# Two square feed-forward layers as seven half-size products instead of eight, in float32 on one Trainium2 core

## The chip, the core and the metric

The kernel runs on one NeuronCore of a Trainium2 chip. The core has five engines with a queue each: TensorE (PE, matrix products into PSUM), VectorE (DVE), ScalarE (ACT), GpSimd (POOL) and SyncE (SP, here only an issuer of DMAs). PE's weight loads have a row of their own in the profile (PEld). The metric is the device time of one execution in microseconds, median over runs.

## What is computed

One transformer block on x of 4 batches x 1024 tokens x 256 features, everything in float32. First attention with 16 heads of 16, its output normalised and added to x. Then the feed-forward part, which the change is about:

```python
def _tlin(x, w, s):
    return jnp.einsum('bsi,oi->bso', x, w) * s
h = jax.nn.silu(_tlin(x, w1_w, w1_s)) * _tlin(x, w2_w, w2_s)      # 256 -> 1024
h = jax.nn.gelu(_tlin(h, h1_w, h1_s), approximate=False)          # 1024 -> 1024
h = jax.nn.gelu(_tlin(h, h2_w, h2_s), approximate=False)          # 1024 -> 1024
return _tlin(h, w3_w, w3_s)                                       # 1024 -> 256
...
x = x + _layernorm(_L0_ffn_ref(_layernorm(x, axis=-1), ...), axis=-1)
```

The weights of these layers are drawn from -1, 0 and 1; the scales `*_s` are real, one per output feature. h1 and h2 are the two square layers.

## The kernel before

**Two programs.** `tile_fast` computes everything on two assumptions, that the attention scores are bounded and that the weights survive a rounding; it counts violations in `misses`, and if there is one, `tile_general` computes all again. With the inputs here the flag stays zero.

**Numbers in two halves.** [...] So an activation is split into a high part (the rounded value) and a low part (what is left), and each product is made twice, with the high and the low part, into the same PSUM accumulator. The weights are rounded once: `round_weights` (L241) loads a block of a weight matrix on POOL's DMA queue, casts it on POOL and stores it to a DRAM copy `rounded`, during attention. Later `check_weights` and `count` (L905, L916) load the original weights again, compare them on DVE with the rounded ones in SBUF and count differences; `judge` (L930) adds the counts up with a 1-column matmul on PE.

**Order.** The schedule is manual: every engine runs its instructions in the order in which the program writes them. Attention is a loop over score tiles (`exponentials`, L464, and `weigh`, L474). Work beside it is cut into `Step`s, kept in chains of the object `side`; each call of `side.take()` (L638) lets each chain run the steps that are due, where `gap` is the number of calls since the chain's last step.

**Feed-forward.** `feed_forward` (L945) goes over the eight half batches of 512 tokens, features on the partitions:
- `gated` (L816): for each of 8 blocks of 128 features, 8 matmuls for w1 and w2, then silu on ACT (L828), the product on DVE (L830), the split on ACT and DVE (L818, L819).
- `gelu_layer` (L838), once for h1 and once for h2: for each pair of output blocks, 8 input blocks x 2 x (high, low) = 32 matmuls through `product` (L812 to L814), then per block of 128 x 512 one gelu on ACT from PSUM (L850), a cast and a difference on DVE (L851, L852). Results go from one pair of buffers (`ha`) to the other (`hb`) and back.
- `finish` (L854): 64 matmuls of 256 columns with w3 (L867), scaled on DVE (L869). Its normalisation and the store to DRAM are a chain of steps taken during the next half batch.
- `prepare` (L782): the norm of the next half batch and its transposes on PE, in steps during h1 and h2.

All of h1, h2, w1, w2 and w3 stay in SBUF for the whole feed-forward part: h1 in the tiles that held attention's stacks, h2 and w3 where attention's other buffers were (`load_weights`, L755; `open_ffn`, L759). PSUM has three buffers of 128 x 1024 for the products, one for attention's accumulator, one for small things.

Of the kernel before, what the change touches and what calls it, by code (L numbers as in the profile page):

```python
# [39 lines left out]
TPQ = NQ // P  # L40

# [76 lines left out]
def tile_fast(ctx: ExitStack, tc: tile.TileContext, x, wqk, wv, wo, w1, w1s, w2, w2s, h1, h1s, h2, h2s, w3, w3s, out, bad):  # L118
# [46 lines left out]
    blocks = [(n, c) for n, w in weights.items() for c in range(0, w.shape[0] // P, rows_at_once[n])]  # L165
    counts = sum(w.shape[0] * w.shape[1] for w in weights.values()) // (P * NQ)
    misses = const.tile([P, counts + B * 2], F32, name="misses")
    nc.vector.memset(misses, 0.0)
    rounded = {n: dram.tile(list(w.shape), F32R, name=f"{n}_r") for n, w in weights.items()}
# [11 lines left out]
    with ExitStack() as actx, ExitStack() as rctx:  # L181
# [62 lines left out]
        def round_weights(n, c):  # L244
# [15 lines left out]
            return [Step(load, 2, False), Step(cast, 4, False)]  # L260

# [439 lines left out]
        def unit_end(b, g, h):  # L701
# [19 lines left out]
            if b == B - 1 and g == NG - 2:  # L721
                side.add([Step(lambda c=c: load_weights("h1", [c]), 2 if c else 0, False) for c in range(HC // 2)])
# [8 lines left out]
            if g == NG - 3 and b + 1 < B:  # L731
                later["chain"][0].extend(later["rest"])
            elif g == NG - 3:
                chunks = [(n, [c]) for n in ("w1", "w2") for c in range(DC)]
                loads = [Step(lambda n=n, c=c: load_weights(n, c), 2 if n == "w1" else 1, False) for n, c in chunks]

                loads[0].ready = lambda: not later["flags"][0]
                loads[DC].ready = lambda: not outstanding
                side.add(loads)
                side.add([Step(lambda: None, 7, False)] + prepare(0, to_vector))  # L740
# [5 lines left out]
        x_in = [t.rearrange("p (c n) -> p c n", c=DC) for t in spare[0:2]]  # L746
        homes = {"w1": spare[2:4], "w2": spare[4:6], "h1": [stacks[w, i, u] for i in range(2) for u in range(2) for w in range(2)]}
        homes["w3"] = [t[:, D * j : D * (j + 1)] for t in spare[6:8] for j in range(HC // 2)]
        halves_of = [(b, h) for b in range(B) for h in range(NH)]
        ffn = {}  # L750

        def halves(pool, name):
            return [pool.tile([P, HC, NQ], F32R, name=f"{name}_{k}") for k in ("hi", "lo")]
# [4 lines left out]

        def open_ffn():  # L759
# [3 lines left out]
            ffn["b"] = halves(fb, "hb")  # L763
            homes["h2"] = [fb.tile([P, HID], F32R, name=f"h2_{c}") for c in range(HC)]
            load_weights("h2")
            load_weights("w3")

# [14 lines left out]
        def prepare(n, copy):  # L782
# [16 lines left out]
            def transposes(c):  # L799
                def run():  # L800
# [3 lines left out]
                    hi, lo = (t[:, c, :] for t in x_in)  # L804
# [7 lines left out]
        def product(p, n, m, i, c):  # L812
            for k, half in enumerate(i):
                nc.tensor.matmul(p, homes[n][c][:, m * P : (m + 1) * P], half[:, c, :], start=c == 0 and k == 0, stop=c == len(homes[n]) - 1 and k == 1)  # L814

        def gated(o, every):  # L816
            def split(m, sg):
                nc.scalar.copy(o[0][:, m, :], sg)  # L818
                return lambda: nc.vector.tensor_sub(o[1][:, m, :], sg, o[0][:, m, :].bitcast(F32))  # L819

            before = None
            for m in range(HC):
                p = ps.tile([P, 2, NQ], F32, tag="big", name="pg")
                for k, n in enumerate(("w1", "w2")):
                    for c in range(DC):
                        product(p[:, k, :], n, m, x_in, c)
                sg = both.tile([P, NQ], F32, tag="o", name="sg", bufs=2)
                nc.scalar.activation(sg, p[:, 0, :], AF.Silu, scale=scales["w1"][:, m : m + 1])  # L828
                low = split(*before) if before else None
                nc.vector.scalar_tensor_tensor(sg, p[:, 1, :], scales["w2"][:, m : m + 1], sg, ALU.mult, ALU.mult)  # L830
                if low:
                    low()
                before = m, sg
                if m % every == every - 1:
                    side.take()
            split(*before)()

        def gelu_layer(o, i, n):  # L838

            for m0 in range(0, HC, 2):  # L840
                p = ps.tile([P, 2, NQ], F32, tag="big", name="ph")
                for c in range(HC):
                    for j in range(2):
                        product(p[:, j, :], n, m0 + j, i, c)
                    if c % 2:
                        side.take()
                for j in range(2):
                    m = m0 + j
                    a = both.tile([P, NQ], F32, tag="o", name="a", bufs=2)
                    nc.scalar.activation(a, p[:, j, :], AF.Gelu, scale=scales[n][:, m : m + 1])  # L850
                    nc.vector.tensor_copy(o[0][:, m, :], a)  # L851
                    nc.vector.tensor_sub(o[1][:, m, :], a, o[0][:, m, :].bitcast(F32))  # L852

        def finish(n, i):  # L854

            b, h = halves_of[n]
            st = {}
            z = both.tile([P, TPQ, D], F32, tag="y", name=f"z_{n}", bufs=1)

            pairs = [ps.tile([P, 2, NQ], F32, tag="big", name="pz") for _ in range(TPQ // 2)]  # L860
            p = [pairs[t // 2][:, t % 2, :D] for t in range(TPQ)]
            for t0 in range(0, TPQ, 2):
                ts = range(t0, t0 + 2)
                for c in range(HC):
                    for t in ts:
                        for k, half in enumerate(i):
                            nc.tensor.matmul(p[t], half[:, c, t * P : (t + 1) * P], homes["w3"][c], start=c == 0 and k == 0, stop=c == HC - 1 and k == 1)  # L867
                for t in ts:
                    nc.vector.tensor_mul(z[:, t, :], p[t], w3s_sb)  # L869
                if n == len(halves_of) - 1:  # L870

                    ln = norms.stats([z[:, t, :] for t in ts])
                    for j, t in enumerate(ts):
                        norms.apply(z[:, t, :], z[:, t, :], ln, j)
                        nc.vector.tensor_add(z[:, t, :], z[:, t, :], xs[b][:, h * TPQ + t, :])
                        for at, tokens in pieces(h, out[b].rearrange("(t p) d -> p t d", p=P)):
                            k = h * TPQ + t - at.start
                            if 0 <= k < at.stop - at.start:
                                nc.sync.dma_start(out=tokens[:, k, :], in_=z[:, t, :])
            if n == len(halves_of) - 1:  # L880
                return []

            def apply(i0):
                def run():
                    for t in range(i0, i0 + 2):
                        norms.apply(z[:, t, :], z[:, t, :], st["ln"], t)
# [3 lines left out]
            def add(t):  # L890
                def run():
                    nc.vector.tensor_add(z[:, t : t + 2, :], z[:, t : t + 2, :], xs[b][:, h * TPQ + t : h * TPQ + t + 2, :])
# [391 lines left out]
```

## Time and profile before

| | us |
|---|---|
| median of 3 runs (1292.04 to 1293.14) | 1292.86 |
| span of the profiled execution | 1291.6 |
| attention, up to the first `pg` matmul | 617 |
| one half batch of the feed-forward part, 780.7 to 862.4 | 81.7 |
| from the last half batch's first matmul (1197.4) to the end | 94.2 |

How to read it: the span is from the first to the last instruction of one profiled execution. Busy time on PE overlaps between neighbouring matmuls, since they are pipelined, so stage lengths are taken from starts, not from busy times. The counts matter too: 2048 matmuls with the square weights (names `ph`), 512 with w1 and w2 (`pg`), 512 of half width with w3 (`pz`), and in the feed-forward part 128 gelus of 128 x 512 on ACT. The DMA rows: 16 loads and 16 stores of 512 KB on POOL's queue for h1 and h2, and 16 loads of 512 KB from the rounded copies on SP's queue.

### The profile page before, as it was taken

Reading aid. Unit: us, or ns where it says so; the run is one execution under the profiler, and the core shown is the slowest. Engines: PE = TensorE matmul, PEld = TensorE weight load, DVE = VectorE, ACT = ScalarE, POOL = GpSimd, SP = SyncE. Lnnn points to the kernel's source line nnn. Section 1 sums busy time; section 2 is a strip of 40 time slices with the busy share of each in tenths; the row PEclk is TensorE's granted clock in tenths of the full one; section 3 lists DMA queues with packets and bytes.
Section 4 is the critical chain, followed back from the end, with each engine's and each line's share of the span. In section 5 each row is a group of like instructions: output and inputs, shape, how many; then the busy total and the mean of one; then the engine's idle time right before and its main releaser. Section 6 shows DMA issues by size and latency. Waiting matters only on the chain.

```text
span 1291.6 us, 21098 instructions
## 1 busy us (share of the span) xinstructions
PE 1244.4 (96%) x8104; PEld 770.0 (60%) x8104; DVE 729.1 (56%) x1625; ACT 699.2 (54%) x855; POOL 120.2 (9%) x166
## 2 busy tenths in 40 slices
PE   7999999999999999998999999999999999999995
PEld 3333334333333334333788888888888888888885
DVE  3466557765677556755643725637456374463533
ACT  3788788888889888998421413214132141331410
POOL 6211012111121110000000000000000000000000
PEclk8999899999999999999999999999999999999998
DMA  4676644665574654462320000201102011020000
GB/s 130 159 188 161 146 121 119 145 162 122 117 178 117 154 117 100 99 163 85 134 92 1 25 1 1 74 17 41 49 1 66 25 42 49 1 66 9 17 1 20
DMA packets 65679, 107.03 MB, mean 83 GB/s; under 512 B 12960, under 2 KB 39200, under 8 KB 65568
## 3 DMA queue, kind: packets, MB, share of 16 engines
q1 hardware_dynamic: 57680, 80.93, 25.4%
q0 software_dynamic: 7360, 24.12, 6.0%
q8 instruction: 66, 1.08, 0.4%
q10 hardware_dynamic: 528, 0.52, 0.2%
q14 instruction: 45, 0.37, 0.1%
HBM read 48.38 MB, written 23.59 MB: 56 GB/s over the span
## 4 chain that ended last, share of the span: by engine, by line
PE 76%; DVE 10%; ACT 8%; issue 2%; DMA 2%; SPq 1%; ACTq 0%; POOL 0%; POOLq 0%; DVEq 0%
PE ph L814 36%; PE acc L479 13%; PE s L471 8%; ACT e L472 6%; PE pz L867 4%; PE p L265 4%; PE pg L814 3%; PE py L265 2%; PE pv L265 2%; DVE sg L830 2%; DVE top L488 2%; DVE ha_lo L819 1%; DVE st L96 1%; PE po L518 1%; ACT sg L828 1%
## 5 line engine op out<-in xcount | busy, mean ns | idle before, releaser
L472 ACT ACTIVATE e<-s 128x1024 f32<-128x1024 f32 x512 | 482.6, 1035 | 59.4 <-PE s L471 49.7
L479 PE MATMUL acc<-e,vaug 128*32 128x512 f32 x2048 | 256.8, 604 | 1.4 <-POOL vaug L449 1.3
L850 ACT ACTIVATE a<-ph,h_scale 128x512 f32<-128x512 f32 x128 | 81.0, 685 | 301.4 <-PE ph L814 301.4
L471 PE MATMUL s<-sq,sk 64*128 64x512 f32 x1024 | 186.0, 443 | 18.2 <-ACT e L472 13.4
L814 PE MATMUL ph<-hb_hi,h 128*128 128x512 f32 x512 | 199.5, 390 | 0.0
L814 PE MATMUL ph<-hb_lo,h 128*128 128x512 f32 x512 | 199.4, 389 | 0.0
L471 PEld LDWEIGHTS s<-sq,sk 64*128 64x128 f32 x1024 | 86.1, 185 | 139.0 <-ACT e L472 114.6
L488 DVE TENSOR_TENSOR top<-top,e 128x512 f32<-128x512 f32 x192 | 134.8, 702 | 16.0 <-ACT e L472 10.8
L106 POOL TENSOR_TENSOR rstd<-ve,minus_half 128x4 f32<-128x4 f32 (+1 forms) x33 | 38.3, 1162 | 834.9 <-DVE ve L104 834.9
L479 PEld LDWEIGHTS acc<-e,vaug 128*32 128x32 f32 x2048 | 49.3, 109 | 107.1 <-issue 102.8
L814 PEld LDWEIGHTS ph<-hb_lo,h 128*128 128x128 f32 x512 | 96.1, 188 | 20.1
L814 PEld LDWEIGHTS ph<-hb_hi,h 128*128 128x128 f32 x512 | 96.1, 188 | 20.2
L851 DVE CAST ha_hi<-a 128x512 fp32r<-128x512 f32 x64 | 27.1, 423 | 142.7 <-ACT a L850 142.7
L814 PE MATMUL ph<-ha_hi,sq 128*128 128x512 f32 x256 | 101.8, 398 | 0.4
L814 PE MATMUL ph<-ha_lo,sq 128*128 128x512 f32 x256 | 99.8, 390 | 0.0
L814 PE MATMUL ph<-ha_lo,sk 128*128 128x512 f32 x256 | 99.7, 390 | 0.0
L814 PE MATMUL ph<-ha_hi,sk 128*128 128x512 f32 x256 | 99.7, 389 | 0.0
L828 ACT ACTIVATE sg<-pg,w_scale 128x512 f32<-128x512 f32 x64 | 43.3, 688 | 56.0 <-DVE ha_lo L819 45.6
L830 DVE SCALAR_TENSOR_TENSOR sg<-pg,w_scale,sg 128x512 f32<-128x512 f32 x64 | 47.1, 745 | 46.3 <-ACT sg L828 46.1
L851 DVE CAST hb_hi<-a 128x512 fp32r<-128x512 f32 x64 | 27.0, 422 | 71.5 <-ACT a L850 71.5
L265 PE MATMUL p<-xT,wqk_sb 128*32 128x512 f32 x512 | 62.3, 608 | 2.9 <-DVE on L496 1.7
L814 PEld LDWEIGHTS ph<-ha_hi,sq 128*128 128x128 f32 x256 | 48.1, 188 | 13.1 <-DVE sg L830 3.4
(165 smaller groups left out, 1640.7 us busy)
## 6 DMA issues: line engine op xcount, KB each, us to landing
w<-in_h_dram POOLq DMA_DIRECT2D x16, 512.0 KB, 5.6
h_r<-wr POOLq DMA_DIRECT2D x16, 512.0 KB, 3.8
x<-in_h_dram SPq DMA_DIRECT2D x32, 256.0 KB, 2.7
top_d<-top SPq DMA_DIRECT2D x30, 256.0 KB, 2.3
folded<-top_d SPq DMA_DIRECT2D x30, 256.0 KB, 3.3
sk<-ck1hi SPq DMA_DIRECT2D x64, 64.0 KB, 2.7
sk<-ck1lo SPq DMA_DIRECT2D x64, 64.0 KB, 2.9
sq<-cq1hi SPq DMA_DIRECT2D x64, 64.0 KB, 2.6
```

The costliest lines, as they stand in the source:

```text
L106: nc.gpsimd.tensor_tensor(rstd[:, :n], ve[:, :n], self.minus_half[:, :n], ALU.pow)
L265: nc.tensor.matmul(o[j : j + SLOT, :], w[:, j : j + SLOT], i, **flags)
L471: nc.tensor.matmul(s[:, a, :], stacks[1, g % 2, u][r, c * P : (c + 1) * P], stacks[0, g % 2, u][r, h * NQ : (h + 1) * NQ], start=True, sto ...
L472: nc.scalar.activation(pair(k)[:, u], s, AF.Exp)
L479: nc.tensor.matmul(acc[SLOT * i : SLOT * (i + 1), :], vaug[g % 2][:, c, i, :], pair(k)[:, i // 2, i % 2, :], start=c == 0, stop=c == NT - 1)
L488: nc.vector.tensor_max(top, top if c > 1 else pair(k - 2)[:, :, :, 0:P], pair(k)[:, :, :, 0:P])
L814: nc.tensor.matmul(p, homes[n][c][:, m * P : (m + 1) * P], half[:, c, :], start=c == 0 and k == 0, stop=c == len(homes[n]) - 1 and k == 1)
L828: nc.scalar.activation(sg, p[:, 0, :], AF.Silu, scale=scales["w1"][:, m : m + 1])
L830: nc.vector.scalar_tensor_tensor(sg, p[:, 1, :], scales["w2"][:, m : m + 1], sg, ALU.mult, ALU.mult)
L850: nc.scalar.activation(a, p[:, j, :], AF.Gelu, scale=scales[n][:, m : m + 1])
L851: nc.vector.tensor_copy(o[0][:, m, :], a)
L867: nc.tensor.matmul(p[t], half[:, c, t * P : (t + 1) * P], homes["w3"][c], start=c == 0 and k == 0, stop=c == HC - 1 and k == 1)
```

## The change

A square layer is seen as a 2 x 2 matrix of blocks, weights A (512 x 512 each) and activations B (512 features x 512 tokens each), over tiles of 1024 tokens, a whole batch. Seven products of sums of blocks replace the eight products of blocks. With s1 = A21 + A22, s2 = s1 - A11, s3 = A11 - A21, s4 = A12 - s2 there are seven weight factors.

- **Weight factors.** `round_corners` replaces `round_weights` for h1 and h2: 16 blocks, each loaded in two DMAs, three quarters copied and four sums made on POOL, stored as seven factors of 1 MB per layer in DRAM (`factors`). They don't stay in SBUF: `load_factor` brings one factor (two loads of 512 KB on SP's queue) into a ring of `SLOTS` = 4 in the tiles that held h1. It is called after each product for the product four later, 56 times in all.
- **Activations.** Eleven blocks of 128 x 4 x 512 are handed out and returned by a list (`Block`, `free`). `Operand.split(i)` makes high and low parts of half a block, 1024 wide: a copy on ACT and a difference on DVE.
- **A layer** (`layer`): seven products k, each in two groups r of 16 matmuls. Two input sums are made on DVE and two on POOL. Products 0 and 1, products 2, 3 and 4, and products 5 and 6 add up in the same PSUM tile, which is read after each. What follows a group, in this order: `evacuate`, the `steps` (input sums, splits of the later operands), the `after` list (splits of this layer's results for the next), one `side.take()`.
- **Around it.** `gated` and `finish` work on 1024 tokens; the gate's result is kept unsplit and split later. The norms of both halves of the next batch are prepared during the layers of this one. The weights are checked against an int8 copy made on POOL, in blocks of 1024 in two chains after the second batch; `judge` is called before the last batch's `finish`.

```diff
-    blocks = [(n, c) for n, w in weights.items() for c in range(0, w.shape[0] // P, rows_at_once[n])]
+    square = ("h1", "h2")
+    blocks = [(n, c) for n, w in weights.items() if n not in square for c in range(0, w.shape[0] // P, rows_at_once[n])]
+    corners = [(n, c, x) for n in square for c in range(HC // 2) for x in range(2)]
...
+            def plain():
+                r = work.tile([P, WIDE], F32R, tag="wr", name="wr", bufs=1)
+                nc.gpsimd.tensor_copy(r[:, 0:half], st["w"][:, 0:half])
+                nc.gpsimd.tensor_copy(r[:, half : 3 * half], st["w"][:, 2 * half : 4 * half])
+                store(r, 0, 3)
+
+            def sums():
...
+                nc.gpsimd.tensor_tensor(s1, a21, a22, ALU.add)
+                nc.gpsimd.tensor_tensor(s2, s1.bitcast(F32), a11, ALU.subtract)
+                nc.gpsimd.tensor_tensor(s3, a11, a21, ALU.subtract)
+                nc.gpsimd.tensor_tensor(s4, a12, s2.bitcast(F32), ALU.subtract)
+                store(r, 3, 7)
...
+            return [Step(load, 2, False), Step(plain, 3, False), Step(sums, 1, False)]
...
+        order = (0, 1, 4, 5, 2, 3, 6)
+        def load_factor(q):
+            if q >= B * 2 * len(order):
+                return
+            n, k = square[q // len(order) % 2], order[q % len(order)]
+            for i, t in enumerate(ring_of[q % SLOTS]):
+                nc.sync.dma_start(out=t.bitcast(F32), in_=factors[n][k, :, 2 * i : 2 * i + 2, :].bitcast(F32))
...
+            def split(self, i):
+                if i == 0:
+                    self.hi, self.lo = Block("hi", F32R), Block("lo", F32R)
+                hi, lo, raw = (t.part(i) for t in (self.hi, self.lo, self.raw))
+                nc.scalar.copy(hi, raw)
+                nc.vector.tensor_sub(lo, raw, hi.bitcast(F32))
...
+        def layer(q, x, pairs, scale, after, late):
+            b11, b21, b22, b12 = (x[i, j] for i, j in ((0, 0), (1, 0), (1, 1), (0, 1)))
+            t2 = Block("t2")
+            moving = [pairs[0, 0], pairs[1, 0], Operand(t2), Operand(b12), Operand(b21), Operand(b11), Operand(b22)]
...
+            def gelu(o, i, m0, src=None):
+                for j in range(2):
+                    m = HC // 2 * i + m0 + j
+                    nc.scalar.activation(o.t[:, m0 + j, :], (o.t[:, m0 + j, :] if src is None else src[:, j, :]), AF.Gelu, scale=scale[:, m : m + 1])
...
+            def evacuate(k, r, p):
+                m0 = 2 * r
+                if k == 0:
...
+                    nc.scalar.copy(out["s"].part(r), p)
+                elif k == 1:
...
+                    gelu(out[0, 0], 0, m0, p)
+                elif k in (2, 3):
...
+                    nc.vector.tensor_add(out[n].part(r), p, out["s"].part(r))
+                else:
+                    n, i, j = (("s", 1, 0), ("v", 1, 1), ("u", 0, 1))[k - 4]
+                    out[i, j] = out[n]
+                    nc.vector.tensor_add(out[n].part(r), p, out[n].part(r))
+                    gelu(out[n], i, m0)
...
+            make1, make2 = sums(nc.vector, b11, b12, b11), sums(nc.vector, t2, b22, b11)
+            make3, make4 = sums(nc.gpsimd, b12, b22, b12), sums(nc.gpsimd, b21, b21, t2)
+            steps = {-1: [lambda: make1(0), lambda: make2(0)], 0: [lambda: make1(1), lambda: make2(1)]}
+            for g in range(4):
+                steps.setdefault(g, []).append(lambda g=g: (make3, make4)[g // 2](g % 2))
+            for k in range(2, 7):
+                for i in range(2):
+                    steps.setdefault(2 * k - 3 + i, []).append(lambda k=k, i=i: moving[k].split(i))
...
+            for k in range(7):
+                start = k in (0, 2, 5)
+                for r in range(2):
+                    if start:
+                        last[r] = ps.tile([P, 2, NQ], F32, tag="big", name="ph")
+                    p = last[r]
+                    for c in range(HC // 2):
+                        for j in range(2):
+                            w = ring_of[q % SLOTS][c // 2][:, c % 2, (2 * r + j) * P : (2 * r + j + 1) * P]
+                            for n, half in enumerate((moving[k].hi, moving[k].lo)):
+                                nc.tensor.matmul(
+                                    p[:, j, :], w, half.t[:, c, :],
+                                    start=start and c == n == 0, stop=c == HC // 2 - 1 and n == 1, skip_group_check=True,
+                                )
+                    if r:
+                        moving[k].release()
+                        load_factor(q + SLOTS)
+                        q += 1
+                    evacuate(k, r, p)
+                    for run in steps.get(2 * k + r, ()):
+                        run()
+                    for run in after.get(2 * k + r, ()):
+                        run(out)
                     side.take()
...
+                after = splits([(9, 0, 0, 0), (11, 0, 0, 1), (12, 1, 0, 0), (14, 1, 0, 1)])
...
+                x = gated(after)
...
+                if b + 1 < B:
+                    chain[0].extend(prepare(2 * b + 2, to_scalar) + prepare(2 * b + 3, to_scalar))
+                q = 2 * 7 * b
+                middle = splits([(11, 0, 0, 0), (12, 0, 0, 1), (13, 1, 0, 0)])
+                x = layer(q, x, dict(pairs), scales["h1"], middle, [])
+                late = [lambda x=x: split(1, 0, 1, x)]
+                ready = dict(pairs)
+                ending = splits([(10, 0, 0, 0), (11, 0, 0, 1), (11, 1, 0, 0), (12, 1, 0, 1), (13, 1, 1, 0), (13, 1, 1, 1)], True)
+                x = layer(q + 7, x, ready, scales["h2"], ending, late)
+                until(lambda: not chain[0])
+                if last:
+                    side.flush()
+                    side.add(judge())
+                    side.flush()
+                rest = [lambda x=x, r=r: split(0, 1, r, x) for r in range(2)] + [x[0, 1].release]
+                chain = finish(b, pairs, {0: rest})
+                if b == 1:
+                    for k in range(2):
+                        side.add(sum(checks[k::2], []))
             side.flush()
```

## The prediction

> **What bounds the kernel now.** I read the slices of the page first, to see the stages. The lines below are the busy tenths of each engine in 40 slices of 32.3 us.
>
> ```profile
> PE   7999999999999999998999999999999999999995
> ...
> DVE  3466557765677556755643725637456374463533
> ACT  3788788888889888998421413214132141331410
> ...
> PEclk8999899999999999999999999999999999999998
> ```
>
> The reader is to see two halves. Up to slice 19 (attention, until about 617 us) ACT and PE are both nearly full. After it (feed-forward) PE alone is full, at full clock, and ACT and DVE have room. All of the change's arithmetic lies in the second half.
>
> Then I asked for the busy time by stage; each of these windows is one half batch of 512 tokens (columns: length, then busy us and count for PE, weight load, DVE, ACT, POOL, then clock, DMA share, GB/s).
>
> ```profile
> 780.70:862.40 81.70, 81.64 (x394) 68.36 (x393) 44.02 (x100) 23.47 (x36) 2.29 (x2) 1.00 0.12 36
> 862.40:944.20 81.80, 81.74 (x395) 68.45 (x394) 44.03 (x100) 23.48 (x36) 2.29 (x2) 1.00 0.11 36
> ```
>
> PE has no gap at all; a half batch is 81.7 us. The busy time of a matmul (390 ns) overlaps its neighbours, so its real price is read from the chain of waits, which gives start, length and count of a merged stretch:
>
> ```profile
> 820.72 41.79 PE ph L814 x184
> 862.51 7.68 PE pz L867 x64
> 870.19 3.67 PE pg L814 x16
> ```
>
> 41.79 / 184 is 0.227 us; the single rows lie 0.2266 apart (689.62, 689.84, 690.07 ...). I use 0.2266 for 512 columns and 7.68 / 64 = 0.12 for 256.
>
> Last, the rows by line, for what DVE and ACT pay:
>
> ```profile
> L850 ACT ACTIVATE a<-ph,h_scale 128x512 f32<-128x512 f32 x128 | 81.0, 685 | 301.4 <-PE ph L814 301.4
> ...
> L852 DVE TENSOR_TENSOR hb_lo<-a,hb_hi 128x512 fp32r<-128x512 f32 x64 | 44.3, 692 | 2.3
> ...
> L818 ACT CAST ha_hi<-sg 128x512 fp32r<-128x512 f32 x64 | 39.2, 612 | 3.8 <-DVE sg L830 3.8
> ...
> L869 DVE TENSOR_TENSOR z<-pz,w3s_sb 128x256 f32<-128x256 f32 x32 | 12.1, 419 | 27.4 <-PE pz L867 27.4
> ```
>
> ACT idles 301 us before the gelus: post-processing waits for PE, never the reverse.
>
> [...] DVE and POOL take turns here, and the POOL copy takes 1.00 us in place of its usual 0.61, the cast 1.49 in place of 1.03.
>
> ```profile
> 181.79 1.70 DVE L488 TENSOR_TENSOR top<-top,e 128x512 f32<-128x512 f32 x2
> ...
> 181.94 1.00 POOL L449 COPY vaug<-cv 128x512 f32<-128x512 f32 x1 [23.95 <-DVE cv L271]
> ...
> 182.89 1.49 POOL L257 CAST wr<-w 128x1024 fp32r<-128x1024 f32 x1
> ```
>
> [...] in the gated stage ACT's 0.69 us silu sits idle 0.8 to 1.3 us behind DVE's `ha_lo`, in program order.
>
> **The change part by part.**
>
> *Removed.* Per layer and batch, 2 halves x 8 x 8 x 2 = 256 matmuls become 7 x 4 x 4 x 2 = 224. Four batches, two layers: 256 fewer, 256 x 0.2266 = 58.0 us, all on the path. Gated and last products keep their counts.
>
> *Weight stream.* Each product needs 1 MB in two 512 KB loads, ring of four, refilled as a product ends: three products ahead, 3 x 7.25 = 21.8 us. Needed: 1 MB per 7.25 us, 145 GB/s. When SP issued the twelve h2 and w3 loads together the window 643 to 648 us carried 408 GB/s, and a 512 KB load landed 5.3 us (median) after its issue. SP's queue now holds these loads between output stores and check loads, each of which waits for one DVE instruction; worst of those waits is a few us beyond its emission. Hidden: 0 us.
>
> *Weight sums, in attention.* 16 blocks of h1/h2 were one load, one 1.1 us cast, one store on POOL. Each becomes two loads (0.55 us to issue), copies, four 256-wide sums [...], two stores[...]. The head copies behind them (`vaug`) are made a whole head group ahead. [...] I take 1 us, bounds 0 and 6; there is no way to gain.
>
> *Post-processing.* Now 14 groups of 16 matmuls per layer, each 16 x 0.2266 = 3.63 us. Widths double to 1024: by the step from 256 to 512 (0.27 us per 256) a DVE add or difference takes 1.22 us (1.14 when streaming), an ACT copy 0.612 + 0.435 = 1.05, the pair of gelus 1.27 as measured. From product 5 on, one group's work is a ring through two FIFO queues: DVE adds the block from PSUM, ACT runs two gelus on it, behind them ACT copies the next operand's high part, and DVE subtracts it for the low part; the next group's add is queued behind that subtraction. Period: 1.22 + 1.16 (gelus until the copy starts) + 1.05 + 1.14 + 0.08 for hand-overs = 4.65 us against PE's 3.63. Groups 8 to 13 of each layer are all of this kind, since the splits for the next layer follow those of the last operands. So the lag grows by 1.02 us a group, 6.1 us over six. PE reads the second half of an operand 3.63 + 1.8 + 0.23 = 5.66 us after the group whose end issued its split; one turn fits, several do not.
>
> I followed the queues by hand from the end of group 7, each instruction starting at the later of its input and its engine.
> - *End of h1, start of h2, without side work.* The last operand's second half is 1.35 us late; the first product of h2 waits 2.0 for its second half. Then DVE makes the input differences, and POOL's differences [...] stand between: the second product waits 3.2 for the late split, the third 2.05. Sum 8.6; with no turn lost to POOL about 5. I take 7.
> - *With the next batch's norms* (batches 1 to 3): 14 side steps, one per group, exactly fill h1; rows of 0.41 and 0.18 for statistics, 0.41 for the scaling, 0.69 for `L806` add 0.7 to 1.3 us to most turns. Worked the same way, 12.0; bounds 7 and 14, I take 10.
> - *End of h2, start of the last products.* Groups 10, 11, 13 hold two splits: 1.35 + 0.75 there, 2.6 for the second operand of the last products and 2.4 for the one split inside that stage: 7.1. Bounds 4 and 8, I take 6.
> - *Last batch.* The verdict on the weights now comes before its last products. PE's 1-column product waits for a DVE reduction queued behind all of h2's splits, about 12 us after PE is done; nothing can pass it on PE's queue. It takes the place of the 6. Bounds 9 and 14, I take 12. (Before, this sat in the seventh half batch and cost nothing.)
> - *Checks of the weights*, all in batch 3: 22 in two chains in step, so each fourth turn gets two 1.22 us comparisons on DVE and two 1.1 us POOL casts [...]. That batch's gated stage has 25 us of DVE work in 29.4 already. Bounds 0 and 17; I take 8.
> - The start of h1 has room (splits are made groups ahead), gated loses two instructions per block: 0.
>
> Sum: 3 x 10 + 7 + 3 x 6 + 12 + 8 + 1 = 76 us lost, 58 gained, +18. The profiled execution has a span of 1291.6 us, 1.3 below the median of 1292.86: 1309.6 in the span, **1311** in the median. With all low ends (47) 1282, with all high ends (112) 1347.
>
> **Rivals.**
> - *Faster.* The lag does not build up: what decides is the period of the ring. If ACT's copies slip ahead of the gelus, or the turn is under about 3.9 us, the lag is 0.3 a group, each of the eight layer ends costs some 2.5 us and the verdict 5: 25 us, giving 1292.9 - 58 + 25 = **1260**. For it: DVE is only 54% busy in a half batch and ACT 29%. Against: the measured durations and FIFO order. The sign turns where the losses fall under 58.
> - *DVE the bound.* All turns lost to POOL and to the checks: losses 100 to 112, **1341**. For it: in h1 of batch 3, 32 us of layer work, 11 of norms, 8 of checks [...] stand against 51 us of PE.
> - *Stream or sums.* If every product waited for both loads in a row, 2 x 6.5 - 7.25 = 5.75 us x 56 products is 322 us, **1557**; the 408 GB/s speak against. If POOL held up attention by 20 us, **1331**. That the change does not do what it says: the counts above exclude it, unless the check fails and the slow general program runs, a multiple of the time.
>
> **How the numbers follow.** A measurement of this kernel can tell about 0.2% (2.6 us). The forecast case (1296 to 1330) has 0.47, DVE the bound 0.19, stream or sums 0.04, no change 0.05, faster 0.25. That is slower 0.70, same 0.05, faster 0.25. Likeliest case alone: 1296 to 1330. Over all I leave a tenth out at each end: 1270, which cuts the rows with losses under 35 us, and 1342.
>
> **What would show it.** 1792 `ph` matmuls still 0.227 apart confirm the gain. Idle PE ending on a low part at the third operand of a product, around the layer ends, 5 to 14 us per boundary, and a pause of about 12 us before the last batch's last products, confirm the losses; DVE adds that start more than 1 us after their group's end show the ring. The forecast is wrong if PE stays above 97% in the feed-forward half, if waits end on a DMA, or if attention ends later than about 623 us.

## The result: 1358 us, five per cent slower, and the profile after

The changed kernel takes 1358.43 us (median of 4 runs, 1356.91 to 1361.29) against 1293.00 for the kernel before (4 runs, 1292.04 to 1293.32): a ratio of 1.0505, with a 95% interval of 1.0492 to 1.0519. The direction of the forecast was right; the size was not. Of +65 us it foresaw +18, and the time lies above its range. Since 58 us of matmuls did go away, 123 us were lost where 76 had been counted.

The page of the kernel after, busy tenths in 40 slices of 33.9 us:

```profile
PE   7999899999999999989988999889987678899875
...
DVE  3566567865786567565967668776798596685855
ACT  3889788888888889883535435354342434353441
...
PEclk9999899999999999999998999989998889899997
```

The first half is as it was: attention ends at 616.8 us (617.1 before). In the second half no engine stays full. PE falls to 8, 7 and 6 tenths in over half of the slices, DVE rises to 6 to 9 in most, and PE's clock, which had stood at 9 in this half up to the last slice, shows 8 in six slices. An engine that was the bound has turned into one that waits.

Busy time by stage shows where (columns: length, then busy us and count for PE, weight load, DVE, ACT, POOL, then clock, DMA share, GB/s). The lines are the two square layers of batches 1 and 2, then the gated stage, the layers and the last products of batch 3, and the layers of batch 4.

```profile
657.10:779.00 121.90, 113.39 (x466) 89.73 (x467) 89.94 (x88) 52.50 (x65) 27.49 (x10) 0.94 0.34 115
...
828.30:948.10 119.80, 110.37 (x466) 87.29 (x465) 86.83 (x85) 52.51 (x66) 27.84 (x10) 0.97 0.35 116
...
968.50:1003.40 34.90, 30.35 (x130) 23.60 (x129) 33.12 (x57) 14.12 (x19) 8.55 (x9) 1.00 0.36 113
1003.40:1145.70 142.30, 114.12 (x466) 88.58 (x466) 109.66 (x114) 52.60 (x65) 47.84 (x26) 0.93 0.45 151
1145.70:1170.80 25.10, 18.87 (x130) 18.07 (x129) 14.18 (x19) 8.68 (x10) 0.00 (x0) 0.86 0.09 34
...
1199.80:1324.80 125.00, 105.90 (x451) 83.38 (x450) 84.56 (x61) 57.63 (x71) 26.87 (x8) 0.97 0.25 84
```

448 matmuls at 0.2266 are 101.5 us. With the next batch's transposes a pair of layers in which PE hardly waits takes 104.8 us (e10_best, below), and 103.1 without them in batch 4. So the pairs lose 17, 15, 37.5 (batch 3, where the weights are compared) and 22 us. Note that DVE is busy for only 90 of 122 us in batch 1. That speaks for the order in which DVE's work comes, and against its sum, as what holds PE up; the experiments test it.

The waits of PE in the feed-forward part, by line (us in total, times, longest):

```profile
PE ph L979 <- DVE lo L891: 20.4, 17, 5.6
PE fpt L858 <- DVE ck1lo L861: 13.9, 3, 6.9
PE ph L979 <- issue: 12.1, 7, 3.0
PE pn L1103 <- DVE total L1099: 11.4, 1, 11.4
PE pz L1037 <- DVE lo L891: 7.2, 6, 3.5
```

Nothing waits for a DMA. PE waits for low parts (`lo`), for the transposes of the next batch (`fpt`, whose PSUM space a late DVE difference holds), and once for the verdict. The seven waits that the view puts down to "issue" have a cause too: each ends 0.10 us after a DVE add has read the PSUM tile that PE's next product adds to. One of them, on DVE's and PE's rows (PE's last matmul before it started at 874.74):

```profile
875.48 1.21 DVE L949 TENSOR_TENSOR v<-ph,v 128x1024 f32<-128x1024 f32 x1
876.79 0.47 PE L979 MATMUL ph<-hi,sq 128*128 128x512 f32 x1 [1.66 <-issue]
```

Product 6 goes on in the tile of product 5, so a late add stops PE directly. In the kernel before PE waited for less than 1 us in this whole part.

Now the chain of waits in h1 of the second batch, in order of time (start, us, what):

```profile
869.83 0.19 DVE mv L99
870.03 0.02 issue
870.05 0.17 DVE ve L106
870.22 1.14 DVE s L949
871.36 0.02 issue
871.38 1.34 ACT s L929 x2
872.72 0.94 ACT hi L890
873.67 0.02 issue
873.69 1.23 DVE lo L891
874.92 0.64 DVE fxn L116 x2
875.56 1.14 DVE v L949
```

This is the ring of the forecast, and PE isn't on it: add on DVE, two gelus and a copy on ACT, difference on DVE, norm work, next add. The adds start at 870.13, 875.48, 880.83, 885.53 and 890.83 by DVE's own row: a turn of 5.35 us with norm work and 4.70 without, against PE's 3.63 a group.

What the forecast didn't have is in PE's row just after. PE had its last matmul at 886.02 and stands still until a transpose at 890.97:

```profile
890.97 1.11 PE L858 MATMUL fpt<-ident,fxn 128*128 128x128 f32 x4 [4.55 <-DVE ck1lo L861]
891.73 0.78 PE L979 MATMUL ph<-hi,sq 128*128 128x512 f32 x1
892.30 0.63 PE L979 MATMUL ph<-lo,sq 128*128 128x512 f32 x1
892.73 0.63 PE L979 MATMUL ph<-hi,sq 128*128 128x512 f32 x1
```

The matmuls are now 0.43 us apart in place of 0.227. The records of the granted clock show half speed from 890.1 to 897.0 us. So this wait costs more than its own length.

Last, DVE and POOL side by side at the start of a layer of batch 3:

```profile
1009.67 1.22 DVE L953 TENSOR_TENSOR t<-g 128x1024 f32<-128x1024 f32 x1
1009.81 3.36 POOL L953 TENSOR_TENSOR g<-g 128x1024 f32<-128x1024 f32 x1 [3.54 <-DVE g L953]
1010.82 3.44 DVE L953 TENSOR_TENSOR g<-g 128x1024 f32<-128x1024 f32 x1
```

By these rows each waits for the other: POOL's sum takes 3.36 us (1.1 of it behind DVE's `t`), and DVE's next sum takes 3.44 in place of 1.22, blocked for 2.2 while POOL's is under way. POOL's 32 sums average 2.8 to 3.4 us by kind. The differences of product 2's operand (`lo<-t`), which meet them, average 2.55 us where `lo<-v` takes 1.22.

### The profile page after: what moved, and what is told of

It is laid out like the page before. It is cut to its first block, busy times and chain, and to the rows that moved or that the text cites. A ratio compares the mean times of both kernels' runs of the same rounds, so it can differ in the third digit from the quotient of the medians.

```text
span 1355.1 us, 20914 instructions
## 1 busy us (share of the span) xinstructions
PE 1225.8 (90%) x7848; PEld 738.3 (54%) x7848; DVE 925.9 (68%) x1506; ACT 812.4 (60%) x941; POOL 335.5 (25%) x333
## 4 chain that ended last, share of the span: by engine, by line
PE 52%; DVE 21%; ACT 14%; issue 6%; DMA 3%; SPq 2%; POOL 1%; ACTq 0%; POOLq 0%; DVEq 0%
PE ph L979 15%; PE acc L523 12%; PE s L515 8%; DVE lo L891 7%; ACT e L516 6%; PE pg L910 5%; ACT hi L890 3%; PE p L309 3%; PE pz L1037 2%; PE py L309 2%; PE pv L309 2%; SPq L463 2%; DVE x L1089 2%; ACT s L929 2%; ACT v L929 2%
## 5 line engine op out<-in xcount | busy, mean ns | idle before, releaser
L979 PE MATMUL ph<-lo,sk 128*128 128x512 f32 x448 | 179.9, 401 | 18.4 <-DVE lo L891 18.4
L979 PE MATMUL ph<-hi,sq 128*128 128x512 f32 x448 | 182.4, 407 | 13.9 <-issue 12.1
L979 PE MATMUL ph<-lo,sq 128*128 128x512 f32 x448 | 180.6, 403 | 2.0 <-DVE lo L891 2.0
L979 PE MATMUL ph<-hi,sk 128*128 128x512 f32 x448 | 178.8, 399 | 2.0 <-ACT hi L890 1.6
L979 PEld LDWEIGHTS ph<-lo,sk 128*128 128x128 f32 x448 | 85.6, 191 | 43.0 <-DVE lo L891 24.1
L979 PEld LDWEIGHTS ph<-hi,sq 128*128 128x128 f32 x448 | 86.9, 194 | 37.5 <-issue 14.6
L979 PEld LDWEIGHTS ph<-hi,sk 128*128 128x128 f32 x448 | 85.9, 192 | 24.5 <-ACT hi L890 6.3
L979 PEld LDWEIGHTS ph<-lo,sq 128*128 128x128 f32 x448 | 87.0, 194 | 22.1 <-DVE lo L891 3.2
L1037 PE MATMUL pz<-w_sb,lo 128*128 128x256 f32 x256 | 69.6, 307 | 7.2 <-DVE lo L891 7.2
L1037 PE MATMUL pz<-w_sb,hi 128*128 128x256 f32 x256 | 69.3, 306 | 4.6 <-ACT hi L890 4.6
## 6 DMA issues: line engine op xcount, KB each, us to landing
w<-in_h_dram POOLq DMA_DIRECT2D x32, 256.0 KB, 5.9
top_d<-top SPq DMA_DIRECT2D x30, 256.0 KB, 2.3
folded<-top_d SPq DMA_DIRECT2D x30, 256.0 KB, 3.5
```

Of the source, the lines that this page charges most:

```text
L979: nc.tensor.matmul(p[:, j, :], w, half.t[:, c, :], start=start and c == n == 0, stop=c == HC // 2 - 1 and n == 1, skip_group_check=True,)
L1037: nc.tensor.matmul(p[:, j, :D], half.t[:, d, (t0 + j) * P : (t0 + j + 1) * P], homes["w3"][c], start=c == n == 0, stop=c == HC - 1 and n == 1,
```

## The experiments

Three theories stood at the start. *Ring*: the gelus ahead of the copies on ACT's queue make the turn too long. *DVE the bound*: POOL's sums and the comparisons block DVE, in whatever order. *PSUM*: the second transpose of `prepare` waits for its single small bank, and that wait, not the ring, stops PE. The verdict and the clock were to be sized.

### The ring: gelus after the splits (e1_order)

```diff
-                    gelu(out[n], i, m0)
+                    return lambda: gelu(out[n], i, m0)
...
-                    evacuate(k, r, p)
+                    ungated = evacuate(k, r, p)
                     for run in steps.get(2 * k + r, ()):
                         run()
                     for run in after.get(2 * k + r, ()):
                         run(out)
+                    ungated()
```

> The two gelus of products 5 to 7 are issued after the group's splits instead of before them, nothing else. If the ring (DVE add, two gelus, copy, DVE difference) is what makes the losses, a turn no longer holds the gelus: DVE falls from 4.70 us a group (5.3 to 6.0 with norm work) to under 3.63, the second batch's two layers from 119.8 us to 104 to 110, and the time from 1358 to 1300 to 1320. If DVE's amount of work, the turns lost to POOL or the checks make them, under 15 us go: 1343 or more.

Measured: 1279.76 us, ratio to the kernel before 0.9913 (0.9882 to 0.9944). That is 79 us less than the change, with the same instructions in another order, more than the 38 to 58 that were expected, and 0.9% under the kernel before. The same place in the second batch, ACT and DVE rows of the timeline:

```profile
846.25 1.23 DVE L949 TENSOR_TENSOR s<-ph,s 128x1024 f32<-128x1024 f32 x1 [0.29 <-PE ph L980]
847.39 1.22 DVE L891 TENSOR_TENSOR lo<-g,hi 128x1024 fp32r<-128x1024 f32 x1
...
847.51 1.34 ACT L929 ACTIVATE s<-s,h_scale 128x512 f32<-128x512 f32 x2 [5.23 <-DVE s L949]
848.75 1.04 ACT L890 CAST hi<-g 128x1024 fp32r<-128x1024 f32 x1
...
849.98 1.23 DVE L949 TENSOR_TENSOR s<-ph,s 128x1024 f32<-128x1024 f32 x1
```

DVE's `lo` follows its add at once: the `hi` that it needs was made on ACT during the group before. Adds come 3.73 us apart, PE's pace. The copy never needed the add; it only stood behind gelus that did. The gain is more than the boundary terms of the forecast, 3 x 10 + 7 + 3 x 6 = 55, and one reason is seen in the clock: the stretches at half speed in the feed-forward part, its last 30 us left out, fell from eleven to two. Counted by matmuls, 147 of the whole feed-forward part ran at half speed in the changed kernel and 41 do here, some 20 us and some 6 us more than at full speed. So up to 14 of the 79 us are the clock's. POOL's sums and the differences that meet them stayed as long as they were (averages of 2.8 to 3.4 and of 2.56 us).

### The comparison of weights (e2_nochecks)

This kernel leaves out the comparison of the weights with their rounded copies; the verdict adds up the other counts.

```diff
-                if b == 1:
-                    for k in range(2):
-                        side.add(sum(checks[k::2], []))
```

> The comparison of the weights with their int8 copies is left out; the verdict adds up zeros. If the checks cost what the third batch takes more than the second (202.2 against 169.3 us), 33 us go: 1325. At the 8 us of the prediction 1350; if the third batch is long for another reason, no change.

Measured: 1322.72 us, 1.0234 (1.0216 to 1.0252), so the comparisons cost 36 us, more than twice the upper bound of the forecast. The third batch without them, by stage (gated, two layers, last products):

```profile
967.80:996.90 29.10, 29.10 (x131) 24.08 (x130) 23.53 (x45) 14.08 (x19) 2.01 (x2) 1.00 0.11 37
996.90:1116.50 119.60, 109.23 (x466) 86.39 (x465) 88.77 (x85) 52.35 (x65) 27.98 (x10) 0.99 0.37 117
1116.50:1136.80 20.30, 16.41 (x129) 15.47 (x128) 11.87 (x15) 8.67 (x10) 0.00 (x0) 1.00 0.12 41
```

It is 169.0 us, like the second; with them it was 202.3. The 22 comparisons are 30.5 us of DVE, some of it spent blocked, and DVE is not full. A part of the cost comes through POOL's queue, whose waits in batch 3 of the changed kernel were:

```profile
POOL rstd L108 <- DVE ve L106: 117.8, 5, 57.4
POOL whole L1086 <- DMA x<-in_h_dram: 35.4, 8, 14.9
```

The cast to int8 (`whole`) waits at the head of POOL's queue for its load, up to 14.9 us, and behind it stand the input sums that products 3 and 4 need. When the load lands they all run at once and lock DVE: two comparisons in a row at 1096.66 and 1100.02 took 3.43 and 3.35 us. With the sums taken off POOL (e5_dvesums, below) the third batch is still 22 us longer than the second, 188.7 against 166.9, where it was 33 in the changed kernel. So about a third of the excess hangs on POOL's sums. The rest falls to 15 us with the gelus' order changed as well (e6_order_sums), and to 3 when the comparisons are moved and spread out (e10_best).

### The bank of the transposes (e3_bank)

```diff
-                    pt = misc(f"fpt_{n}_{c}")
+                    pt = ps_acc.tile([P, NQ], F32, tag="acc", name=f"fpt_{n}_{c}") if n > 1 and c else misc(f"fpt_{n}_{c}")
```

> The second transpose of each prepared half batch goes to attention's free PSUM bank. If PE's waits of 2.7, 4.7 and 7.0 us before the last transposes of h1 are a price of their own[...], 14 to 24 us go: 1334 to 1344. If they only show DVE's lag, which the next low part would show as well, under 6 us go: 1352 or more.

Measured: 1356.13 us, 1.0492 (1.0475 to 1.0510): 2 us less, which is within the scatter, of the 13.9 that PE spent in that wait. In its trace that wait is gone, and the waits for `lo` have grown from 20.4 to 29.7 us. So the bank was where DVE's lag showed, not a cause. The PSUM theory falls.

### The verdict (e4_verdict)

```diff
+                if last:
+                    side.add(judge())
                 late = [lambda x=x: split(1, 0, 1, x)]
...
-                if last:
-                    side.flush()
-                    side.add(judge())
-                    side.flush()
```

> The verdict's steps start before the last batch's h2 instead of after it. If PE's 11.6 us before the last products are the verdict's alone, they go and 13 us with the cold start after them; since the late splits then show as in the other batches (5 us and more), 5 to 10 us are left: 1348 to 1353. If nothing of it was on the path, 1358.

Measured: 1352.73 us, 1.0462 (1.0445 to 1.0480), 6 us less. The wait of 11.4 us is gone (in the changed kernel the 26 products of 256 columns that followed it, up to 1330.4 us, started 0.21 us apart in place of 0.12, at half speed), and PE waits more for the splits of the last products instead, as the forecast's "takes the place of the 6" had it.

### POOL's sums on DVE (e5_dvesums)

```diff
-            make3, make4 = sums(nc.gpsimd, b12, b22, b12), sums(nc.gpsimd, b21, b21, t2)
+            make3, make4 = sums(nc.vector, b12, b22, b12), sums(nc.vector, b21, b21, t2)
```

> The two input sums that POOL makes at the start of each layer are made by DVE, nothing else. If the turns lost to POOL (DVE differences of 3.4 us in place of 1.22) cost what they seem to, PE's waits at the start of h2 shrink, 4 to 6 us a batch and more with the checks: 1328 to 1342. If DVE's amount of work is the limit, its 4.9 us more per layer make it no faster: 1355 or more.

Measured: 1333.98 us, 1.0339 (1.0316 to 1.0361), 24 us less, though DVE got 32 more instructions of 1.22 us. Each sum on POOL had cost DVE up to 2.2 us of blocking, more than the 1.22 us of doing it. More than half of the 24 us is batch 3's, which goes from 202.2 us to 188.7; there the sums had also stood behind the casts on POOL's queue. For the blocking by itself, the some 11 us of the other three batches are the evidence.

### Both together (e6_order_sums)

The edits of e1_order and e5_dvesums.

> Gelus after the splits, and POOL's two sums on DVE. If the sums' locks still cost the 1.4 us at each start of h2 and most of the third batch's waits, 8 to 16 us go from 1280: 1264 to 1272. If the order alone was the whole of it, 1280.

Measured: 1259.88 us, 0.9762 (0.9747 to 0.9777). The sums are still worth 20 us when the ring is gone (8 to 16 were expected), 14 of them in batch 3, so they are a loss of their own and not a part of the ring. Layers of 104.5 and 104.9 us in batches 1 and 2 leave nothing more to gain there; that of batch 3 has 114.3.

### All four (e7_all)

In addition the verdict of e4_verdict, and the comparisons in one chain:

```diff
-                    for k in range(2):
-                        side.add(sum(checks[k::2], []))
+                    side.add(sum(checks, []))
...
-            return [Step(load, 1, False), Step(cast, 2, False), Step(run, 1, False)]
+            return [Step(load, 1, False), Step(cast, 1, False), Step(run, 1, False)]
```

> Gelus after the splits, POOL's sums on DVE, the verdict before the last h2, and the checks of the weights in one chain with a turn of three steps, spread over the third and the start of the last batch. If the checks' cost is their crowding, the third batch comes near the second (153 us): 1243 to 1256, 3 to 4% under the kernel before. If it is their work as such, it only moves: 1262 or more.

Measured: 1259.34 us, 0.975 (0.9737 to 0.9763): a miss, no gain over e6_order_sums. The layers of batch 3 fell to 108.4 us, but the gated stages of batches 3 and 4 rose to 36.1 and 36.3 us where 29.1 is their length. DVE's waits between 930 and 1130 us say why:

```profile
DVE x L1091 <- POOL whole L1088: 12.2, 4, 3.6
```

With one call between load and cast, the cast still waited for the load, and now the comparison stood at the head of DVE's queue behind it, with the gated products behind that. The wait had only moved from POOL's queue to DVE's.

### How much a stop of PE costs (e8_hold and e9_short)

Both take the kernel before, whose PE never stops, and hold PE up by a 1-column product that waits for a chain of small additions on DVE: e8 at the start of 15 of the 16 square layers, e9 in the middle of a product in all 16 (with another 1-column product and a copy ahead of the additions). Nothing is left out. The edit of e8:

```diff
+        def hold(k):
+            d = both.tile([P, NQ], F32, tag="o", name="hold", bufs=2)[:, 0:16]
+            nc.vector.memset(d, 0.0)
+            for _ in range(6 * k):
+                nc.vector.tensor_add(d, d, d)
+            pn = misc("pn")
+            nc.tensor.matmul(pn[0:1, 0:1], d[:, 0:1], ones, start=True, stop=True)
```

> The kernel before, with PE held up once at the start of each square layer but the first, for k times six small DVE additions, k from 1 to 15, through a one-column product that reads their result; the additions change no output. If idleness alone halves the clock, [...] 3.4 or 6.8 us at half clock, at a price of 1.7 to 3.4 us each beyond the hold. If the drops in the changed kernel came from something else, none follow.

Measured: 1547.28 us in one run, against 1291.28. PE's pauses were 4.83 to 24.2 us, 226.2 in all. The time grew by 256, so a pause cost about 2 us more than itself ((256.0 - 226.2) / 15). A half-speed clock followed each of them.

> Kernel before, with PE held up once in the middle of a product group of each of the 16 square layers, by a 1-column product, a copy and 1 to 23 short additions on DVE, so holds of about 0.7 to 6 us. If the clock halves after any idle time, every hold is followed by matmuls 0.427 us apart. [...]

Measured: 1362.66 us in one run, against 1293.09. The pauses were 0.61, 0.82, 1.03, 1.24, 1.45, 1.87, 2.08 and 2.70 us, after all of which the clock stayed full, and 3.33, 3.54, 3.75, 3.96, 4.16, 4.58, 4.80 and 5.21, after all of which it halved, for 3.4 or 6.8 us. The stretches ahead of, in and after two of them (the 0.50 and 1.00 near the end of a line are the clock):

```profile
686.40:694.90 8.50, 6.45 (x30) 4.98 (x29) 3.87 (x15) 1.27 (x2) 0.00 (x0) 1.00 0.00 0
694.90:701.70 6.80, 5.68 (x15) 4.49 (x16) 1.83 (x8) 1.26 (x2) 0.00 (x0) 0.50 0.00 0
...
1290.70:1293.40 2.70, 0.16 (x4) 0.05 (x4) 2.07 (x12) 0.00 (x0) 0.00 (x0) 1.00 0.00 0
1293.40:1300.20 6.80, 6.80 (x31) 5.63 (x32) 2.15 (x4) 1.27 (x2) 0.00 (x0) 1.00 0.00 0
```

The half-speed stretch begins 1.1 us before the long pause ends; in the 5.7 us of it that are left 15 matmuls start, against 31 in the 6.8 us after the short pause. All pauses together are 45.1 us and the time grew by 69.6, so each of the eight long ones cost about 3 us beyond itself, if the short ones cost no more than themselves.

In this run the limit lies between 2.70 and 3.33 us, but length alone doesn't set it. In the changed kernel a pause of 2.21 us (705.58 to 707.79) was followed by half speed from 709.2 on, and one of 3.22 (1263.65 to 1266.87) was not. What sets the two apart is where they fall. In every trace the records of the clock begin on a grid of 3.41 us (in the changed kernel the half-speed stretches before the last 10 us are one, two and once four times 3.413 us long). The first pause lies within one cell of this grid; the second is cut in two by a grid line at 1265.6. An estimate from the feed-forward parts of all twelve traces, with 0.2266 us (0.427 at half speed) counted as busy for a matmul of 512 columns, and less in proportion for a narrower one: of the cells at full speed, all 72 with more than 2.2 us idle were followed by half speed, none of the 2195 with less than 2.0 was, and six of the 16 between were. In the trace of the changed kernel by itself all 12 with more than 2.1 us idle were, and none of the 182 others, which had less than 1.9. By this estimate a pause of up to 4 us could pass where a grid line halves it, though none over 3.3 us in these traces did. The sharp limit in e9_short owes something to luck.

### The version that is left (e10_best)

From e7_all: the comparisons begin one layer earlier, with two calls between load and cast, and the verdict waits until they are through.

```diff
                 if last:
+                    until(lambda: not compared[0])
                     side.add(judge())
+                if b == 1:
+                    compared = side.add(sum(checks, []))
                 late = [lambda x=x: split(1, 0, 1, x)]
...
-                if b == 1:
-                    side.add(sum(checks, []))
...
-            return [Step(load, 1, False), Step(cast, 1, False), Step(run, 1, False)]
+            return [Step(load, 1, False), Step(cast, 2, False), Step(run, 1, False)]
```

> Order of the gelus, sums on DVE and the verdict as in e7_all, but the comparison of weights begins before the second layer of the second batch, one chain, with two calls between load and cast, so that no DVE instruction should wait for a cast that waits for its load. If that wait made the gated stages of batches 3 and 4 36 us long, they come back to 29 to 31 and the time is 1243 to 1251 us. If the comparisons cost what they cost wherever they stand, the time stays at 1256 to 1262.

Measured: 1244.15 us (5 runs, 1241.19 to 1248.54), 0.9623 (0.9603 to 0.9644). The page's slices and, by stage, the second batch (gated, layers, last products) and the gated stage and layers of the third:

```profile
PE   7999999999999999998999999999999999999995
...
PEclk8999899999999999999999999999999999999998
```

```profile
775.20:804.30 29.10, 29.10 (x131) 24.07 (x130) 23.53 (x45) 14.11 (x19) 2.01 (x2) 1.00 0.11 37
804.30:909.10 104.80, 104.80 (x466) 85.59 (x465) 89.20 (x101) 54.76 (x69) 6.75 (x6) 1.00 0.47 153
909.10:924.30 15.20, 15.20 (x130) 15.20 (x129) 9.98 (x14) 6.37 (x8) 0.73 (x1) 1.00 0.40 127
924.30:953.60 29.30, 29.30 (x131) 23.95 (x130) 27.74 (x51) 14.09 (x19) 8.45 (x7) 1.00 0.28 90
953.60:1060.90 107.30, 105.59 (x466) 85.43 (x465) 97.05 (x112) 54.64 (x70) 10.30 (x9) 1.00 0.50 164
```

PE is full again, with DVE busy for 89 of 105 us, and its clock drops nowhere in the feed-forward part before the last 10 us. Of the 58 us that seven products in place of eight take away, 49 arrive. DVE has all the sums and comparisons, and PE waits for it for some 4 us in all. So DVE's amount of work was never the bound.

## Why the prediction was wrong in size, step by step

**Right.**
- *Removed, 58.0 us.* 1792 `ph` matmuls remain, and where PE runs at full clock they are 0.227 apart. The profile of e10_best, 1239.0 us against 1291.6, shows 52.6 of it.
- *Weight stream, 0.* A 512 KB load landed 3.7 and 4.4 us (medians of the two halves) after its issue, and PE waited for none.
- *Weight sums in attention, 1.* Attention ended 0.3 us earlier, which is within the scatter between executions.
- *The ring.* Forecast 4.65 us, measured 4.70; with norm work 0.7 to 1.3 more, measured 5.35 to 6.0. It was the largest cause, as e1_order shows.
- *The verdict, 12.* PE waited 11.4; net of what it covers, 6.

**Wrong: the step "Checks of the weights", "Bounds 0 and 17; I take 8".** e2_nochecks gives 36. The forecast counted instructions: two comparisons and two casts each fourth turn. It didn't follow what it had asked for elsewhere, what is queued behind an instruction that waits. The cast waits for a load on POOL's queue, and the sums for products 3 and 4 wait behind the cast. By e5_dvesums that is about a third of the third batch's excess over the second; the rest went with the gelus' order and with the comparisons spread out (in e10_best the third batch takes 151.8 us against 149.1). The term is 28 of the 47 us that are missing (123 - 76), and by itself it takes the time out of the likeliest case, which ended at 1330.

**Too small: the terms for the ends of the layers.** Against the stages of e10_best (29.1, 104.8 and 15.2 us, first gated stage 40.4, last layers 103.1), batches 1 and 2 lost 22.2 and 20.1 us where 10 + 6 were counted. Batch 4 lost some 22 where 7 + 12 were. Batch 3 without its comparisons lost 20, again for 16. That is 17 us too few in all. Walking the queues by hand had given 12.0 + 7.1 = 19.1 for a batch, nearer than what was then taken; the deduction "with no turn lost to POOL about 5. I take 7" had no row behind it. Three things were missing or too small:
- *The shared PSUM tile.* The walk had PE wait for low parts only. That a product can't go on in a tile before DVE has read it was counted as nothing; PE stood 12.1 us for it, in seven waits.
- *The clock.* It had PE at full speed after each wait. By the records, 147 matmuls of the feed-forward part ran at half speed in the changed kernel, some 20 us more than at 0.2266 (0.12 for the narrow ones). e8_hold and e9_short show that pauses alone bring this about; in the changed kernel it wasn't taken away by itself.
- *POOL's locks.* One sum takes an estimated 2.3 us without the waiting (3.36 us less 1.1; the shortest of the 32 took 2.40). The forecast's price for one was not shown by any row of the kernel before. That DVE loses its turns too was in the walk (8.6 us with them, about 5 without), but the terms taken kept only a part of it. e5_dvesums puts POOL's sums at 24 us over eight layers, and e6_order_sums at 20 without the ring, more than half of it in batch 3 beside the casts.

These shares overlap: order, sums and comparisons gave 79, 24 and 36 us when each was undone alone, 139 in all, more than the 123 that were lost.

**The rivals.** "DVE the bound", 1341, was nearer in size, and its two sources, locks and comparisons, were the ones under-priced. That DVE's amount of work is the limit is refuted: e10_best gives DVE more instructions and is 114 us faster. "Faster", 1260, named the right lever ("if ACT's copies slip ahead of the gelus"): the changed kernel didn't do it, e1_order did, and the other losses kept even that at 1280. Neither the stream nor the sums in attention mattered. What also failed is the range: its upper end let the losses reach 107 us, near the 112 of every unknown at its bound, and the bounds themselves were too narrow.

Still open: how the other 65 us of e1_order's 79 divide between waits for low parts, for the shared PSUM tiles and for the transposes; these waits follow from each other. Why attention ends anywhere from 615 to 623 us in the profiles of kernels that share its code is open too. It doesn't touch the 15 us between e7_all and e10_best: their feed-forward parts alone take 638.9 and 623.9 us, and 13 of these 15 us lie in the gated stages of batches 3 and 4.

## What to carry to other kernels

When a post-processing path alternates between two in-order queues, write down its turn and compare it with the producer's period. Then issue first what the other queue is waiting for, and last what nobody waits for soon (here the gelus, 79 us). Don't let an instruction that may wait for a load stand ahead of work that is due, on any queue: moved from POOL's queue to DVE's, the same wait still cost 15 us (e7_all against e10_best). And when pauses are added up, count the longer ones (from 2.2 us on some did it here, from 3.3 on all) with 2 to 3 us on top for the clock.

## What the runs showed of the hardware

- The clock follows a grid of 3.41 us: a cell of it in which PE is idle for more than about 2.2 us is followed by half speed (72 of 72 in these traces, and none of 2195 under 2.0), for one or two cells where the pauses are short. In e9_short this took in all pauses of 3.33 us and more and none of 2.70 or less. A longer pause costs no more beyond itself: in e8_hold half speed ended 3.1 to 6.2 us after the pause, 3.2 after the shortest (4.83 us) and 4.9 after the longest (24.2).
- DVE and POOL, both on two-input sums of 1024 columns, take turns one by one: 3.4 us each, in place of 1.22 (DVE) and some 2.3 (POOL, estimated as 3.36 less 1.1 of waiting). Moving POOL's sums to DVE took 24 us off the time, some 11 of them where nothing else stood on POOL's queue.
